# Picking two gathered rows per step by matmul from the first step to the last double step

## The chip, the cores and the metric

The kernel runs on one core of one Trainium2 chip. The metric is the device time of one execution in microseconds. Three runs of the kernel before took 1789.95 to 1790.13 us, with a median of 1790.06 us.

The core has five engines with their own instruction queues: TensorE (PE; its weight loads are listed apart as PEld), VectorE (DVE), ScalarE (ACT), GpSimd (POOL) and the SyncE queue (SP), which here only issues DMAs.

## The reference

A graph has N = 6250 nodes with 64 features and E = 206,250 edges, sorted by destination. There are four heads of 16 features.

```python
Qh = (x @ Wq.T + bq).reshape(n, H, D)
Kh = (x @ Wk.T + bk).reshape(n, H, D)
Vh = (x @ Wv.T + bv).reshape(n, H, D)
Ee = (edge_attr @ We.T + be).reshape(-1, H, D)
score = (Kh[src] * Qh[dst] * (1.0 / np.sqrt(D)) * Ee).sum(-1)
score = jnp.exp(jnp.clip(score, -5.0, 5.0))
msg = Vh[src] * score[..., None]
wV = jax.ops.segment_sum(msg, dst, num_segments=n)
out = _layernorm(x + wV.reshape(n, H * D), axis=-1)
```

Since the edges are sorted by destination, queries and sums are local. The sources are random, so k and v of each edge's source have to be fetched row by row.

## The kernel before, in words

**Tiles and steps.** 128 edges make a tile, one edge per partition; there are T = 1612 tiles. Eight tiles make a group (G = 8), 202 groups in all, the last with four tiles. `STEPS` cuts the groups into NS = 105 steps: 97 steps of two groups (16 tiles), then eight steps of one group.

**Where k and v of the sources come from.** There are four ways.

- Most tiles are gathered: `gather_kv` (line 400) issues one indirect DMA on POOL's queue for each tile, which reads 128 rows of the table `kv_tab` in DRAM.
- The first four groups (XG = 4, the tiles of steps 0 and 1) are gathered from x itself (line 230) while the tables are still being computed. The loop of line 370 then transposes them (L375), copies them to SBUF (L378) and multiplies them with the weights of k and v (L380, L382, L384).
- Of every sixth step from step 12, one tile is fetched row by row over SP's queue (`fetch_rows`, line 528).
- The last two tiles of a double step are *picked* by matmul. x lies in SBUF as three bf16 parts whose sum is the f32 value (`parts`, 50 blocks of 128 partitions). In step s, for both picked tiles of step s + 2, `sources` (line 460) writes a row of source numbers (ScalarE), `sources_turned` (469) transposes it on PE, `hots` (476) compares it on VectorE with the block numbers and so makes 50 one-hot matrices in two halves, and `picks` (486) multiplies them with the parts, 25 matmuls per half, so 100 in a step. In step s + 1, `picked` (494) adds the three parts, and `picked_turned` and `picked_kv` (502, 510) make k and v of the picked rows and write them into the step's buffer. The kernel before picks in steps 4 to 94 (`picks_in`, with M0 = 4 and LAST = NS - 11).

**Where the parts come from.** `table_parts` and `table_parts_rest` (444, 454) load x in blocks of eight over SP and split them on ScalarE and VectorE in the steps 0 to 3, after a memset of the whole tile (L427).

**Buffers of k and v.** `kvs` has KVB = 5 buffers, one per step in turn. In step s, after its message, `gather(s + 4)` is called. Step s + 5 uses the same buffer as step s, so the first of its gathers has to wait until the message of step s has read it. The gathers of groups 4 to 7 (steps 2 and 3) are issued ahead of the loop (line 406).

**The rest of a step.** The order on each engine is the order of the calls, written out by hand in the loop of line 708. `products` multiplies k with the queries and with the edge values (L602, L603), `scores` reduces, clips and exponentiates (L609, L611, L612), `message` multiplies v with the score (L619), `minus` splits the message into three bf16 parts (L622, L630, L632), `queries(s + 1)` (L595) makes the next step's queries, and `sums` (L638) and `add` (L652) collect the messages per destination in the next step. All PSUM tiles of the loop have one buffer each.

**The end.** When the last sums are there, `last_add` (693) adds them to the last block of 128 nodes; the layer norm of a block is `spreads`, `roots`, `scales` and `norm`. In the kernel before, `scales` and `norm` of the block before the last stand ahead of `last_add`.

The fallback behind `branch.Else()` for unsorted or widely spread destinations doesn't run with these inputs.

Of the kernel before, what the change touches and what calls it, by code (L numbers as in the profile page):

```python
# [37 lines left out]
CB = 10  # L38
KVB = 5
XG = 4  # L40
TB = 8
M0 = 4
PAD = N
SPARE = N + 1
TABLES = 4
# [8 lines left out]
def tiles_in(s):  # L54
    return sum(tiles_of(g) for g in groups_of(s))


def groups_of(s):
    return range(STEPS[s][0], STEPS[s][0] + STEPS[s][1])
# [1 line left out]

LAST = NS - 8 - 3


def picks_in(s):
    return M0 <= s <= LAST

# [31 lines left out]
def tile_gnn(ctx: ExitStack, tc: tile.TileContext, x, xT, wT, bias, beT, weT, eT, src, dst, dst_rows,  # L103
# [16 lines left out]
    def kv_of(g):  # L120

        s = max(s for s in range(NS) if STEPS[s][0] <= g)
        j = (g - STEPS[s][0]) * G
        return kvs[s % KVB][:, j:j + G, :]
# [29 lines left out]
    be_p = consts.tile([3, G, C], BF16, name="be_p")  # L154
    wkv = consts.tile([P, 2, 2 * C], F32, name="wkv")
    bkv_p = consts.tile([3, G // 2, 2 * C], BF16, name="bkv_p")
    minus_b = consts.tile([P, P], BF16, name="minus_b")

    acc = consts.tile([P, RING, 4, C], F32, name="acc")
# [24 lines left out]
    with tc.tile_pool(name="nodes", bufs=1) as nodes, \  # L184
# [182 lines left out]
            fetch_queries(g)  # L367


        for g in range(XG):  # L370
            for h in range(2):
                tp = npsum.tile([P, 2, P], F32, name="tp", bufs=2)
                for u in range(2):
                    j = 4 * h + 2 * u
                    nc.tensor.transpose(tp[:, u, :],  # L375
                                        XS[g][:, j:j + 2, :].rearrange("p j c -> p (j c)"), ident)
                xe = nodes.tile([P, 2, P], F32, name="xe", bufs=2)
                nc.scalar.activation(xe, tp, AF.Copy)  # L378
                pv = npsum.tile([P, 4, 2 * C], F32, name="pv", bufs=2)
                nc.tensor.matmul(pv, ones_b, bkv_p, start=True, stop=False, skip_group_check=True)  # L380
                for u in range(2):
                    nc.tensor.matmul(pv[:, 2 * u:2 * u + 2, :], xe[:, u, :], wkv, start=False,  # L382
                                     stop=u == 1, skip_group_check=True)
                nc.scalar.activation(kv_of(g)[:, 4 * h:4 * h + 4, :], pv, AF.Copy)  # L384

    def edge_values(pe, et, n):

# [6 lines left out]
    def keys(t0):  # L394

        n = min(KEYS, T - t0)
        nc.vector.tensor_scalar(key_i[:, :n], dst_i[:, t0:t0 + n], P - 1, None, op0=OP.bitwise_and)
        nc.vector.tensor_copy(key[:, t0:t0 + n], key_i[:, :n, None].to_broadcast([P, n, 2]))

    def gather_kv(g, j):  # L400
        t = g * G + j
        nc.gpsimd.indirect_dma_start(  # L402
            out=kv_of(g)[:, j, :], out_offset=None, in_=kv_tab[:, :],
            in_offset=bass.IndirectOffsetOnAxis(ap=src_i[:, t:t + 1], axis=0))

    for g in range(XG, 2 * KVB - 2):
        for j in range(G):
            gather_kv(g, j)

    rv = nc.values_load(n_wide[0:1, 0:1], min_val=0, max_val=NR2 * 4)  # L410

    with tc.If(rv == 0) as branch:

        with tc.tile_pool(name="work", bufs=2) as work, \
# [8 lines left out]
            pa = small[:, 4 * C:7 * C].rearrange("p (i c) -> p i c", i=3)  # L423
            nc.tensor.transpose(col, row_b[:, 0:1].to_broadcast([P, P]), ident_b)

            parts = accp.tile([P, NB, 3, C], BF16, name="parts")
            nc.vector.memset(parts, 0.0)  # L427
            NX = N // NB
            x_v = x.rearrange("(p b) c -> p b c", p=NX)
            n_picks = LAST - M0 + 1  # L430
            src_f = accp.tile([P, n_picks, 2], F32, name="src_f")
            t0 = (M0 + 3) * 2 * G - 2
            for i in range(2):
                nc.vector.tensor_copy(src_f[:, :, i],
                                      src_i[:, t0 + i:t0 + i + 2 * G * (n_picks - 1) + 1:2 * G])
            pick = fixed.tile([P, 4 * P], F32, name="pick")
            rows3 = pick[:, :6 * C].rearrange("p (k i c) -> p k i c", k=2, i=3)
            HOT, FAR, X = {}, {}, {}
# [2 lines left out]

                return ap.rearrange("p (a b) -> p a b", b=2)

            def table_parts(b):

                n = min(TB, NB - b)
                raw = work.tile([P, TB, C], F32, name="raw", bufs=1)
                nc.sync.dma_start(raw[:NX, :n], x_v[:, b:b + n, :])
                rest = pick[:NX, :n * C].rearrange("p (b c) -> p b c", b=n)
                nc.scalar.activation(rest, raw[:NX, :n], AF.Copy)  # L450
                nc.scalar.activation(parts[:NX, b:b + n, 0], raw[:NX, :n], AF.Copy)
                return rest

            def table_parts_rest(b, rest):
                n = min(TB, NB - b)
                nc.vector.tensor_sub(rest, rest, parts[:NX, b:b + n, 0])
                nc.scalar.activation(parts[:NX, b:b + n, 1], rest, AF.Copy)
                nc.vector.tensor_sub(parts[:NX, b:b + n, 2], rest, parts[:NX, b:b + n, 1])

            def sources(s, i):  # L460

                if picks_in(s):
                    FAR[s, i] = work.tile([P, P], BF16, name="far")
                    nc.scalar.activation(FAR[s, i], row50, AF.Identity,
                                         bias=src_f[:, s - M0, i:i + 1], scale=-1.0)

            def sources_turned(s, i):
                if picks_in(s):  # L470
# [39 lines left out]
            def picked_kv(s):  # L510
                if picks_in(s):
                    xe, kv = X.pop(s)
                    nc.tensor.matmul(kv, ones_b, bkv_p[:, :2], start=True, stop=False,
                                     skip_group_check=True)
                    nc.tensor.matmul(kv, xe, wkv, start=False, stop=True, skip_group_check=True)  # L515
                    nc.scalar.activation(kvs[(s + 2) % KVB][:, 2 * G - 2:, :], kv, AF.Copy)

            def gather(s):
                for g in groups_of(s):
                    for j in range(tiles_of(g)):  # L520
                        if is_rowed(s) and (g - STEPS[s][0]) * G + j == COLUMN:
                            continue
                        if not picks_in(s - 2) or g == STEPS[s][0] or j < G - 2:
                            gather_kv(g, j)

            RS, RK = {}, {}
# [53 lines left out]
            def onehot_edges(s):  # L580

                n, t0 = tiles_in(s), STEPS[s][0] * G
                OH[s] = work.tile([P, 2 * G, P], BF16, name="of")
                shape = [P, n, P // 2, 2]
                nc.vector.tensor_tensor(OH[s].rearrange("p t (a c) -> p t a c", c=2)[:, :n],  # L585
                                        pairs(col)[:, None].to_broadcast(shape),
                                        key[:, t0:t0 + n, None, :].to_broadcast(shape),
                                        op=OP.is_equal)
# [95 lines left out]
            def scales(lo, hi):  # L684
                nc.vector.reciprocal(rstd[:, lo:hi], rstd[:, lo:hi])

            def norm(b):
                nc.vector.tensor_scalar(y[:, b, :], y[:, b, :], stats[:, b, 0:1], rstd[:, b:b + 1],
                                        op0=OP.subtract, op1=OP.mult)
                n = P if b < BIG else REST  # L690
                nc.sync.dma_start(out[b * P:b * P + n, :], y[:n, b, :])
# [6 lines left out]
                                               op0=OP.mult, op1=OP.add)  # L698

            closed, scaled, normed = 0, 0, 0  # L700
            keys(0)
            for k, g in enumerate(groups_of(0)):
                onehot_rows(g, spread(g))
# [1 line left out]
                edges(0, k)  # L705
            queries(0)
            onehot_edges(0)
            for s in range(NS):
                more = s + 1 < NS
                for g in groups_of(s):  # L710
# [13 lines left out]
                sources_turned(s + 1, 0)  # L724
                if nexts[1:]:
                    onehot_rows(nexts[1], spread(nexts[1]))
                making = [b for b in range(s * 2 * TB, (s + 1) * 2 * TB, TB) if b < NB]
                if making:
                    rest = table_parts(making[0])
                prod = products(s)  # L730
                picked(s - 1)
                if more:
# [36 lines left out]
                if more:  # L769
# [9 lines left out]
                    for _ in range(3):  # L779
                        if normed < scaled:  # L780
                            norm(normed)
                            normed += 1
                for i, b in enumerate(making):
                    if i:
                        rest = table_parts(b)
                    table_parts_rest(b, rest)
            assert normed == B - 2
            sums(NS - 1)
            roots(B - 2, B - 1)
            close(B - 1)  # L790
            scales(B - 2, B - 1)
            norm(B - 2)
            last_add(NS - 1)
            spreads(B - 1)
            roots(B - 1, B)
            scales(B - 1, B)
            norm(B - 1)

    with branch.Else():

        sums = [dram.tile([NR, C], F32, name=f"sums{i}") for i in range(TABLES)]
        with tc.tile_pool(name="gconsts", bufs=1) as gc, \
                tc.tile_pool(name="gloads", bufs=3) as loads, \
                tc.tile_pool(name="ggath", bufs=4) as gath, \
                tc.tile_pool(name="gwork", bufs=2) as work, \
                tc.tile_pool(name="gpsum", bufs=2, space=bass.MemoryType.PSUM) as psum:
            zeros = gc.tile([P, NB * C], F32, name="zeros")
# [25 lines left out]
            def gather(g, j):  # L833
                if j == 0:
                    Q[g] = gath.tile([P, G, C], F32, name="gq")
                t = g * G + j
                if g >= 2 * KVB - 2:
                    gather_kv(g, j)
                nc.gpsimd.indirect_dma_start(
                    out=Q[g][:, j, :], out_offset=None, in_=q_tab[:, :],  # L840
                    in_offset=bass.IndirectOffsetOnAxis(ap=dst_i[:, t:t + 1], axis=0))
# [121 lines left out]
```

## Time and profile before

| what | value |
|---|---|
| median of three runs | 1790.06 us |
| the profiled execution | 1789.88 us, span 1788.0 us |
| PE busy / weight loads | 1638.5 us (92%) / 1369.6 us |
| DVE busy | 1481.6 us (83%) |
| ACT busy | 914.0 us (51%) |
| POOL busy | 1337.4 us (75%) |
| mean granted PE clock | 0.951 of full |
| kv gathers on POOL (L402) | 1383 of 944 ns |
| pick matmuls (L491) | 9100, 828.3 us busy in all |
| one-hot compares (L481) | 364 of 1813 ns |

The span runs from the first to the last instruction of the profiled execution; the execution's own time is 1.9 us longer. A row of the slices divides the span into 40 parts of 44.7 us and gives the busy share of each in tenths. In a group of instructions, the figures behind the first bar are total busy time and mean length in ns, and behind the second the engine's idle time just before them with what ended most of it. In the waits, the figures are total us, times, and the longest. Rows of the timeline begin with the start and the length in us; an idle time before the instruction and its releaser stand in brackets. Matmuls overlap, so their busy times add up to more than PE is really occupied.

### The profile page before, as it was taken

Reading aid. Unit: us, or ns where it says so; the run is one execution under the profiler, and the core shown is the slowest. Engines: PE = TensorE matmul, PEld = TensorE weight load, DVE = VectorE, ACT = ScalarE, POOL = GpSimd, SP = SyncE. Lnnn points to the kernel's source line nnn. Section 1 sums busy time; section 2 is a strip of 40 time slices with the busy share of each in tenths; the row PEclk is TensorE's granted clock in tenths of the full one; section 3 lists DMA queues with packets and bytes.
Section 4 is the critical chain, followed back from the end, with each engine's and each line's share of the span. In section 5 each row is a group of like instructions: output and inputs, shape, how many; then the busy total and the mean of one; then the engine's idle time right before and its main releaser. Section 6 shows DMA issues by size and latency. Waiting matters only on the chain.

```text
span 1788.0 us, 44286 instructions
## 1 busy us (share of the span) xinstructions
PE 1638.5 (92%) x15751; PEld 1369.6 (77%) x15751; DVE 1481.6 (83%) x1695; ACT 914.0 (51%) x1328; POOL 1337.4 (75%) x1427
## 2 busy tenths in 40 slices
PE   8978999999999998999999899999989998999864
PEld 8647888888888787787887778777877887787632
DVE  6459999999998898888889888888988888898654
ACT  3465555555554464454455445455544554455443
POOL 7777777777777777777777777777777777777774
PEclk9968999999999999999999999999999999999855
DMA  7443333333333333332333333323332333333331
GB/s 221 132 121 84 90 93 94 93 94 92 93 81 94 93 86 89 92 94 80 93 93 81 93 81 93 92 81 99 87 93 80 94 93 81 93 90 81 91 80 44
DMA packets 109970, 166.71 MB, mean 93 GB/s; under 512 B 69196, under 2 KB 71452, under 8 KB 109626
## 3 DMA queue, kind: packets, MB, share of 16 engines
q0 software_dynamic: 45280, 91.78, 19.4%
q1 hardware_dynamic: 64074, 71.01, 14.1%
q8 instruction: 125, 2.05, 0.5%
q10 hardware_dynamic: 384, 1.00, 0.3%
q14 instruction: 107, 0.88, 0.2%
HBM read 156.33 MB, written 7.33 MB: 92 GB/s over the span
## 4 chain that ended last, share of the span: by engine, by line
PE 38%; POOL 29%; issue 14%; DVE 13%; DMA 4%; ACT 3%; DVEq 0%; SPq 0%; POOLq 0%; ACTq 0%
POOL kv L402 29%; PE pick L491 18%; PE pe L391 5%; DVE hot L481 5%; DMA kv<-kv_tab,src_i 3%; PE pq L630 2%; PE small L638 2%; DVE prod L603 2%; DVE prod L602 2%; PE pb L555 2%; PE pe L388 2%; PE pb L515 1%; PE pq L595 1%; DVE pq L619 1%; PE ps L350 1%
## 5 line engine op out<-in xcount | busy, mean ns | idle before, releaser
L402 POOL DMA_INDIRECT kv<-kv_tab,src_i x1383 | 1305.3, 944 | 421.7 <-issue 399.8
L491 PE MATMUL pick<-parts,hot 128*128 128x192 bf16 x9100 | 828.3, 249 | 0.0
L491 PEld LDWEIGHTS <-hot 128*128 128x128 bf16 x9100 | 771.7, 99 | 38.1
L481 DVE TENSOR_TENSOR hot<-small,block 128x3200 bf16<-128x3200 bf16 x364 | 645.3, 1813 | 0.4 <-PE pick L491 0.4
L572 ACT ACTIVATE to<-pb,minus_row 126x1024 bf16<-126x1024 f32 x202 | 222.7, 1102 | 371.0 <-PE pb L555 367.2
L632 ACT ACTIVATE msg<-pq 128x1024 bf16<-128x1024 f32 (+2 forms) x210 | 207.6, 989 | 222.3 <-PE pq L630 222.3
L391 PEld LDWEIGHTS pe<-we_sb,et 128*128 128x128 f32 x1612 | 209.7, 203 | 133.4 <-issue 95.3
L602 DVE TENSOR_TENSOR prod<-kv,pq 128x1024 f32<-128x1024 f32 (+2 forms) x105 | 123.5, 1176 | 169.3 <-DMA kv<-kv_tab,src_i 52.0
L391 PE MATMUL pe<-we_sb,et 128*128 128x128 f32 x1612 | 250.3, 302 | 0.0
L577 ACT ACTIVATE to<-to,one_p 126x1024 bf16<-126x1024 bf16 x202 | 230.6, 1142 | 3.5
L638 PEld LDWEIGHTS <-of 128*128 128x128 bf16 x1612 | 145.3, 102 | 31.1 <-issue 7.9
L638 PE MATMUL small<-msg,of 128*128 128x192 bf16 x1612 | 161.9, 257 | 0.5 <-ACT msg L632 0.5
L388 PE MATMUL pe<-be_p,ones_b 3*128 3x512 bf16 x202 | 79.7, 395 | 86.3 <-DVE prod L603 86.1
L630 PE MATMUL pq<-msg,minus_b 128*128 128x512 bf16 x404 | 128.0, 396 | 33.1 <-ACT msg L622 19.5
L622 ACT ACTIVATE msg<-pq 128x1024 bf16<-128x1024 f32 (+2 forms) x105 | 103.8, 989 | 96.8 <-DVE pq L619 96.8
L609 DVE TENSOR_REDUCE small<-prod 128x64 f32<-128x1024 f32 (+2 forms) x105 | 123.6, 1177 | 14.5 <-PE small L471 8.8
L555 PE MATMUL pb<-key_rows,ident_b 112*128 112x512 bf16 x403 | 127.9, 400 | 2.8 <-ACT to L572 2.8
L603 DVE TENSOR_TENSOR prod<-prod,pe 128x1024 f32<-128x1024 f32 (+2 forms) x105 | 123.6, 1177 | 3.6
L619 DVE TENSOR_TENSOR pq<-kv,small 128x1024 f32<-128x1024 f32 (+2 forms) x105 | 123.4, 1175 | 1.4 <-ACT small L612 1.4
L585 DVE TENSOR_TENSOR of<-small,key 128x2048 bf16<-128x2048 bf16 (+2 forms) x105 | 122.9, 1171 | 0.3
L595 PEld LDWEIGHTS <-to 126*128 126x128 bf16 x1612 | 63.5, 101 | 25.3 <-issue 25.1
L612 ACT ACTIVATE small<-small 128x64 f32<-128x64 f32 (+2 forms) x105 | 21.7, 207 | 111.1 <-DVE small L611 109.2
(129 smaller groups left out, 996.4 us busy)
## 6 DMA issues: line engine op xcount, KB each, us to landing
et<-in_eT SPq DMA_DIRECT2D x100, 512.0 KB
rk<-kv_tab SPq DMA_DIRECT2D x1920, 0.5 KB
kv<-kv_tab,src_i POOLq DMA_INDIRECT x1383
qw<-q_tab SPq DMA_DIRECT2D x202, 15.8 KB
kv_tab<-kv_sb SPq DMA_DIRECT2D x5, 640.0 KB
q_tab<-q SPq DMA_DIRECT2D x5, 480.0 KB
acc<-in_x SPq DMA_DIRECT2D x48, 32.0 KB
out<-y SPq DMA_DIRECT2D x48, 32.0 KB
```

Source lines behind the costliest of these rows:

```text
L391: nc.tensor.matmul(pe[:, 2 * u:2 * u + 2, :], et[:, u, :], we_sb, start=False, stop=u == n // 2 - 1, skip_group_check=True)
L402: nc.gpsimd.indirect_dma_start(out=kv_of(g)[:, j, :], out_offset=None, in_=kv_tab[:, :], in_offset=bass.IndirectOffsetOnAxis(ap=src_i[:, t ...
L481: nc.vector.tensor_tensor(HOT[s, i, h].rearrange("p b (a c) -> p b a c", c=2), pairs(from_b[i])[:, None].to_broadcast(shape), block2[:, bl ...
L491: nc.tensor.matmul(rows3[:, i], hot[:, k, :], parts[:, b], start=b == 0, stop=b == NB - 1)
L555: nc.tensor.matmul(pb[:, b:b + 4, :], ident_b[:NR2, g // 2:g // 2 + 1].to_broadcast([NR2, P]), key_rows[:, g % 2, b * P:(b + 4) * P], star ...
L572: nc.scalar.activation(TO[g][:, :n, :], pb[:3 * W, :n, :], AF.Square, bias=minus_row3[:3 * W])
L577: nc.scalar.activation(TO[g][:, :n, :], TO[g][:, :n, :], AF.Relu, bias=one_p[:3 * W], scale=-1.0)
L602: nc.vector.tensor_mul(prod[:, :n, :], kvs[s % KVB][:, :n, :C], PQ[s][:, :n, :])
L603: nc.vector.tensor_mul(prod[:, :n, :], prod[:, :n, :], PE[s][:, :n, :])
L630: nc.tensor.matmul(msg[:, lo:hi, :], minus_b, M3[s][:, lo:hi, i, :], start=False, stop=True, skip_group_check=True)
L632: nc.scalar.activation(M3[s][:, :n, i + 1, :], msg[:, :n, :], AF.Copy)
L638: nc.tensor.matmul(PA[s], OH[s][:, j, :], M3[s][:, j], start=j == 0, stop=j == n - 1)
```

## The change

Three things change.

1. Picks are made in steps 0 to 96 instead of 4 to 94. The tiles of steps 2 to 5 and of the single-group steps 97 and 98 that were gathered are now picked: two tiles for each of six more steps. `is_picked` decides for the gathers ahead of the loop and in it. The sources of step 0 and the hots of its first tile are made ahead of the loop.
2. The parts of x are made before the loop, in the chunk that computes k and v of the first four groups: x, which lies transposed in SBUF already (`xT_sb`), is transposed back on PE, four blocks at a time, and split on ScalarE and VectorE. In that chunk the rows of the next half group are turned before k and v of the present one are computed. The loads of x over SP, the memset and the splitting inside steps 0 to 3 go.
3. At the end, `last_add`, `spreads` and `roots` of the last block stand ahead of `scales` and `norm` of the block before it.

The changes in the fallback only keep it consistent. The core of the diff:

```diff
-LAST = NS - 8 - 3
+LAST = NS - 8 - 1
 def picks_in(s):
-    return M0 <= s <= LAST
+    return 0 <= s <= LAST
+
+def is_picked(g, j):
+    s = max(s for s in range(NS) if STEPS[s][0] <= g)
+    return picks_in(s - 2) and g == groups_of(s)[-1] and j >= G - 2
...
+        def parts_of_x(b):
+            n = min(TB, NB - b)
+            px = npsum.tile([P, 2, 2 * C], F32, name="ps").rearrange("p i (j c) -> p (i j) c", j=2)
+            px = px[:, :n]
+            for u in range(n):
+                nc.tensor.transpose(px[:, u, :], xT_sb[:C, (b + u) * P:(b + u + 1) * P],
+                                    ident[:C, :C])
+            nc.scalar.activation(parts[:, b:b + n, 0], px, AF.Copy)
+            nc.vector.tensor_sub(px, px, parts[:, b:b + n, 0])
+            halves.append((px, b, n))
+
+        def rest_of_x():
+            px, b, n = halves.pop(0)
+            nc.scalar.activation(parts[:, b:b + n, 1], px, AF.Copy)
+            nc.vector.tensor_sub(parts[:, b:b + n, 2], px, parts[:, b:b + n, 1])
+
+        order = [(g, h) for g in range(XG) for h in range(2)]
+        blocks = list(range(0, NB, TB))
+        xe = x_turned(*order[0])
+        for i, gh in enumerate(order):
+            following = x_turned(*order[i + 1]) if i + 1 < len(order) else None
+            for b in blocks[2 * i:2 * i + 2]:
+                parts_of_x(b)
+            first_kv(*gh, xe)
+            xe = following
+            while halves:
+                rest_of_x()
...
     for g in range(XG, 2 * KVB - 2):
         for j in range(G):
-            gather_kv(g, j)
+            if not is_picked(g, j):
+                gather_kv(g, j)
...
-            parts = accp.tile([P, NB, 3, C], BF16, name="parts")
-            nc.vector.memset(parts, 0.0)
...
-                        if not picks_in(s - 2) or g == STEPS[s][0] or j < G - 2:
+                        if not is_picked(g, j):
                             gather_kv(g, j)
...
             closed, scaled, normed = 0, 0, 0
+            sources(0, 0)
+            sources_turned(0, 0)
             keys(0)
...
             queries(0)
             onehot_edges(0)
+            sources(0, 1)
+            sources(1, 0)
+            for h in range(2):
+                hots(0, 0, h)
             for s in range(NS):
...
-                making = [b for b in range(s * 2 * TB, (s + 1) * 2 * TB, TB) if b < NB]
-                if making:
-                    rest = table_parts(making[0])
...
-                for i, b in enumerate(making):
-                    if i:
-                        rest = table_parts(b)
-                    table_parts_rest(b, rest)
             assert normed == B - 2
             sums(NS - 1)
             roots(B - 2, B - 1)
             close(B - 1)
-            scales(B - 2, B - 1)
-            norm(B - 2)
             last_add(NS - 1)
             spreads(B - 1)
             roots(B - 1, B)
+            scales(B - 2, B - 1)
+            norm(B - 2)
             scales(B - 1, B)
             norm(B - 1)
```

`x_turned` and `first_kv` are the two halves of the old loop body of line 370 (transposes and first copy; matmuls and second copy). `TB`, the blocks split at a time, goes from 8 to 4.

## The prediction

> **What bounds the kernel now.** I read the busy table and the slices first, then the groups, then the waits and the table of windows.
>
> ```profile
> PE 1638.5 (92%) x15751; PEld 1369.6 (77%) x15751; DVE 1481.6 (83%) x1695; ACT 914.0 (51%) x1328; POOL 1337.4 (75%) x1427
> ...
> POOL 7777777777777777777777777777777777777774
> ...
> L402 POOL DMA_INDIRECT kv<-kv_tab,src_i x1383 | 1305.3, 944 | 421.7 <-issue 399.8
> L491 PE MATMUL pick<-parts,hot 128*128 128x192 bf16 x9100 | 828.3, 249 | 0.0
> ```
>
> By share of busy time PE leads. But POOL's digit is 7 in every slice from first to last, as only an engine that never waits has it. The waits explain the missing quarter:
>
> ```profile
> POOL kv L402 <- issue: 399.8, 1311, 0.3
> ```
>
> 1311 times 0.3 us in front of a gather while nothing was outstanding, and never longer: a gather occupies POOL for 0.944 us plus 0.3 us. The first kv gather starts at 43.04 us and the last at 1768.85, so one costs 1725.8/1382 = 1.249 us. POOL is the bound for the whole run; a step with two picks (14 gathers) is 17.5 us long on it. PE's own pace is shorter: where PE has arrears (160 to 366 us) its blocks of picks return every 15.7 us, and later the first product waits for the gather's DMA.
>
> ```profile
> 60.00:80.00 20.00, 19.31 (x48) 10.82 (x48) 2.44 (x1) 6.62 (x13) 15.12 (x17) 1.00 0.33 90
> 100.00:120.00 20.00, 13.62 (x67) 8.75 (x66) 12.73 (x15) 14.72 (x19) 15.12 (x17) 0.65 0.42 120
> 300.00:400.00 100.00, 100.00 (x1056) 85.58 (x1054) 93.55 (x99) 54.07 (x76) 75.54 (x81) 1.00 0.35 93
> ```
>
> Columns: window, length, busy PE, PEld, DVE, ACT, POOL, granted PE clock, DMA share, GB/s. POOL stays at 75.6% whether VectorE does 12% or 94%.
>
> **The change part by part.**
>
> *Gathers.* Picks go from 91 to 97 steps, so POOL loses 6 x 2 = 12 gathers, 15.0 us. Eight lie at the start (tiles of steps 2 to 5), four at the end (steps 97 and 98). The two ends have different covers, so I cost them apart: 8 x 1.249 = 10.0 us and 4 x 1.249 = 5.0 us at most.
>
> *The steps' added work.* Six steps get 100 pick matmuls (25 in 2.06 us: 8.2 us of PE) and four hots (1.81 us each, 7.25 us of DVE). In steps 0 to 3 they take the place of the table's parts, of a 4.06 us memset, and of waits: those steps now start their products at 84.97, 100.98, 117.00 and 133.22, 16.1 us apart, with PE at a clock of 0.61 to 0.65. With picks I give them the 15.7 us of later steps, within POOL's 17.5. So they cost nothing if PE runs at full clock; the rivals price the other case.
>
> A rule speaks against the added hots: the Trainium skill, "SBUF — State Buffer", section "SBUF: two separate sides", says that a VectorE operation in a two-port mode locks GpSimd out of a shared port, so that it can't write descriptors for its DMAs. If each of the 24 new hots held up POOL for its length, 24 x 1.81 = 43 us would be lost. The windows above show the gathers' pace unchanged at 94% VectorE; I take nothing.
>
> *Parts of x between k and v.* These are 50 transposes of 64x128, 13 ScalarE copies and 13 subtractions, twice each. No row shows these transposes. The nearest is the query matmul with the same stationary shape and the same 64 moving columns; from the chain of waits:
>
> ```profile
> 33.58 18.15 PE ps L350 x84
> ```
>
> 0.216 us each, 10.8 us for 50. The other bound is the 128-column transpose of line 375, two in 0.63 us: 0.31 each, 15.7 us. I take 0.216. ScalarE (4 x 0.38 + 0.38 + 0.60 = 2.5 us per half group) and DVE (about 1.7) stay under PE's 4.4. Turning the next half ahead of k and v saves part of this wait:
>
> ```profile
> 58.48 0.60 PE L380 MATMUL pv<-bkv_p,ones_b 3*128 3x512 bf16 x1
> 58.65 0.38 ACT L378 ACTIVATE xe<-tp 128x256 f32<-128x256 f32 x1
> 59.08 1.36 PEld L382 LDWEIGHTS pv<-wkv,xe 128*128 128x128 f32 x4 [0.51 <-ACT xe L378]
> ```
>
> Of the 0.51 us some 0.2 is the bias matmul's own; I take 0.3 x 8 = 2.4 us. So the step loop's prelude starts 8.4 us later (bounds 5 and 15.7). Behind the branch, PE now waits for the first "far" row (source copies, one ScalarE activation, one transpose) ahead of its spread: about 1.55 us. SP loses seven loads of x and only gets freer.
>
> *What is late next.* The gathers of step 5 write the buffer that step 0 read, so they wait for step 0's message:
>
> ```profile
> 90.33 1.23 DVE L619 TENSOR_TENSOR pq<-kv,small 128x1024 f32<-128x1024 f32 x1 [1.36 <-ACT small L612]
> ...
> 103.08 0.94 POOL L402 DMA_INDIRECT kv<-kv_tab,src_i  x1 [0.30 <-issue]
> ```
>
> Now the buffer is free at 91.56 and is wanted at 103.08: 11.5 us of slack. After, it is wanted 6 gathers earlier (2 + 2 + 2), at 43.04 + 42 x 1.25 = 95.6. The message ends at 91.56 + 8.4 + 1.55 - 0.9 (two part copies that stand before exp on ScalarE now) + 0.3 (source transposes in step 0) = 100.9. POOL stalls for 5.3 us, and all gathers behind it are late by that. Step 6 is wanted 17.5 us later, and message 1 should come 15.2 to 15.7 us after message 0: no second stall. Front: -10.0 + 5.3 = -4.7.
>
> *The end.* After step 96 the groups are single and the steps follow the chain product, score, message, two subtractions, queries. Starts of the first product of steps 100 to 104:
>
> ```profile
> 1738.05 0.69 DVE L602 TENSOR_TENSOR prod<-kv,pq 128x512 f32<-128x512 f32 x1 [2.59 <-PE pq L595]
> 1746.68 0.69 DVE L602 TENSOR_TENSOR prod<-kv,pq 128x512 f32<-128x512 f32 x1 [2.59 <-PE pq L595]
> 1756.58 0.69 DVE L602 TENSOR_TENSOR prod<-kv,pq 128x512 f32<-128x512 f32 x1 [4.27 <-PE small L638]
> 1766.65 0.69 DVE L602 TENSOR_TENSOR prod<-kv,pq 128x512 f32<-128x512 f32 x1 [4.72 <-PE small L638]
> 1774.05 0.42 DVE L602 TENSOR_TENSOR prod<-kv,pq 128x256 f32<-128x256 f32 x1 [3.31 <-PE pq L595]
> ```
>
> 8.63 us is the chain's own length (the product waits for queries); only the 9.9 and 10.07 wait for gathers. Earlier gathers can take those two down to 8.6: 2.8 us. The picks of step 96 put about 0.9 us back (a reduction of 0.55 and two k and v matmuls). So the four gathers give -1.9, not -5.0; the rest becomes slack on POOL.
>
> *Last sums first.* The last reduction now waits for another block's root: its table load ends at 1780.44 and the reduction starts at 1781.12, while the last sums on PE ended at 1780.00. Going first gains 1.07; the other block's reciprocal and norm then stand between the last root and its use, 0.3 back: -0.8.
>
> **Sum.** -4.7 - 1.9 - 0.8 = -7.4 us. The span goes from 1788.0 to 1780.6, the profiled execution's 1789.88 to 1782.5; the median of the runs, 1790.06, lies 0.2 above that execution: 1782.7 us.
>
> **Rivals.**
> A, no stall: the transposes cost half (0.107) or hide in gaps, and POOL never waits: -10.0 - 1.9 - 0.8 gives 1777.4; with the full 5.0 at the end, 1774.3. For it speaks that a weight load of line 375's transposes lasts 0.23 us where one of L350 lasts 0.33; against it, the delay would have to be under 3.1 us, and 1.55 of prelude come on top.
> B, no measurable change: 0.31 us per transpose and no gain from turning ahead make 15.7 us, 7.3 more, all stall: 1790.0. Line 375's row speaks for it, its twice as many columns against it.
> C, slower, PE's clock: the Trainium skill, "TensorE: Matmul & The Clock Gate", section "Part 1: The HAM clock gate", says that the array is throttled by default and only sustained activity releases it. At the 0.61 to 0.65 of the window from 100 to 120, the 8.2 us of picks take 13.4, and a step about 20.9, 3.4 over POOL's 17.5; four such steps stall POOL by 13.8 us: 1796.5. It decides from 19.4 us per step (7.4 lost). Against it: when picks begin at 150 us, 25 matmuls take 2.06 to 2.23 us at once, and the clock is 1.00 from 160 on; after the change PE is dense from 51 us on.
>
> **How the numbers follow.** My case has 0.64 (own range 1779.5 to 1786), A 0.13, B 0.14, C 0.09. A measurement of this kernel tells about 0.2% (3.6 us) from no change. Faster: my case, A, and a fraction of B, 0.80. Same: the rest of B and mild C, 0.12. Slower: 0.08. The range takes in A without the full end and most of B: 1776.5 to 1788.5.
>
> **What would show it.** The gather group falls to x1371 at 944 ns, the picks rise to 9700. One wait of POOL of about 5 us, near 96 us, for step 0's message (DVE, the line of the message's product), and none later; the last gather starts near 1768.85 - 15.0 + 5.3 = 1759. The chunk of k and v with transposes takes about 33 us instead of 24.6. PE's clock is near 1.00 between 100 and 140 us, and products come 15.7 us apart from step 0 to step 35 or so. In the last eight steps products wait for queries, none for a DMA. I am wrong if POOL doesn't wait at the start (A), waits repeatedly (C), or if the last product's lag behind the last gather doesn't grow by about 3 us.

## The result: 7.3 us faster, for partly other reasons

The changed kernel takes 1782.72 us (median of five runs, 1778.57 to 1783.07); the kernel before takes 1790.06 (1789.95 to 1790.29). The ratio is 0.9952, 95% interval 0.9938 to 0.9967. The profiled execution took 1782.72 us, its span is 1780.8 us; before it was 1788.0, so 7.2 us of span went. The prediction was 1782.7 us. The total is right, and two of its three terms are not: in this profile they are wrong by 3.3 and 3.7 us in opposite directions.

The busy table, the slices and the groups of the profile after, against the lines shown of before:

```profile
PE 1676.8 (94%) x16437; PEld 1416.1 (80%) x16437; DVE 1522.3 (85%) x1738; ACT 916.8 (51%) x1357; POOL 1326.2 (74%) x1415
...
POOL 7777777777777777777777777777777777777773
PEclk9999999999999999999999999999999999999965
...
L440 POOL DMA_INDIRECT kv<-kv_tab,src_i x1371 | 1294.2, 944 | 420.0 <-issue 395.0
L513 PE MATMUL pick<-parts,hot 128*128 128x192 bf16 x9700 | 882.9, 249 | 0.0
```

The gathers fall from 1383 to 1371 and still take 944 ns each; the picks rise from 9100 to 9700, and POOL keeps its 7 in every slice but the last. The added work on PE and VectorE did not slow a gather.

POOL's own instructions in order of time (start, duration, then in brackets the idle time ahead of it) show the stall that the prediction placed at 95.6 us:

```profile
96.26 0.94 POOL L440 DMA_INDIRECT kv<-kv_tab,src_i  x1 [0.84 <-DVE pq L642]
...
115.14 0.94 POOL L440 DMA_INDIRECT kv<-kv_tab,src_i  x1 [1.71 <-issue]
```

Every other kv gather has 0.30 to 0.32 in the brackets. The first of these is step 5's first gather behind message 0: 0.84 - 0.30 = 0.54 us lost. The second is step 6's first gather, which has to wait for message 1; that message ends on VectorE at 113.16 + 1.22 = 114.38 us. 1.41 us are lost there. The profile names no releaser for it; that it is message 1 follows from the buffers. Together 1.95 us, not 5.3, and at two places, not one. The last gather, before and after:

```profile
1768.85 0.94 POOL L402 DMA_INDIRECT kv<-kv_tab,src_i  x1 [0.30 <-issue]
```

```profile
1756.06 0.94 POOL L440 DMA_INDIRECT kv<-kv_tab,src_i  x1 [0.30 <-issue]
```

It starts 12.8 us earlier (12 gathers are 15.0 us; 15.0 - 1.95 = 13.0).

The end did not follow. The first product of step 96 before, and those of steps 96 to 100 and 104 after the change, on VectorE:

```profile
1696.65 1.22 DVE L602 TENSOR_TENSOR prod<-kv,pq 128x1024 f32<-128x1024 f32 x1 [7.05 <-ACT to L572]
```

```profile
1689.93 1.22 DVE L625 TENSOR_TENSOR prod<-kv,pq 128x1024 f32<-128x1024 f32 x1 [2.61 <-PE small L661]
1703.91 0.69 DVE L625 TENSOR_TENSOR prod<-kv,pq 128x512 f32<-128x512 f32 x1 [2.40 <-PE pick L513]
1714.79 0.69 DVE L625 TENSOR_TENSOR prod<-kv,pq 128x512 f32<-128x512 f32 x1 [3.94 <-ACT kv L539]
1725.34 0.68 DVE L625 TENSOR_TENSOR prod<-kv,pq 128x512 f32<-128x512 f32 x1
1734.54 0.69 DVE L625 TENSOR_TENSOR prod<-kv,pq 128x512 f32<-128x512 f32 x1 [2.49 <-PE pq L618]
...
1767.81 0.42 DVE L625 TENSOR_TENSOR prod<-kv,pq 128x256 f32<-128x256 f32 x1 [3.31 <-PE pq L618]
```

Product 97 waits for PE, which has the picks of step 96, and product 98 for the k and v that those picks make. Both waits are new. The first two of the four blocks of picks of step 96 in the changed kernel, and the queries of step 97 in the kernel without picks at the end (the first of the experiments):

```profile
1693.75 3.88 PE L513 MATMUL pick<-parts,hot 128*128 128x192 bf16 x25
1698.03 2.14 PE L513 MATMUL pick<-parts,hot 128*128 128x192 bf16 x24
```

```profile
1698.39 0.58 PE L618 MATMUL pq<-qw,to 126*128 126x64 bf16 x8 [1.11 <-ACT msg L655]
```

In the changed kernel a third block follows at 1701.36 us, and only then, at 1703.42, the queries of step 97. Without those picks the queries wait for the message alone. From product 96 to the last it takes 77.9 us; before it took 77.4 (1696.65 to 1774.05). So the 7.2 us of span are: product 96 comes 6.72 earlier, the eight steps to the last product are 0.48 longer, and from the last product to the end it is 0.96 shorter (12.99 against 13.95 us). So 10.0 - 1.95 = 8.05 of the front's 10.0 us reach the gathers (7.8 by the last gather's start: 12.8 less the 5.0 of the four gathers at the end), and 6.72 of those reach product 96.

### The profile page after: what moved, and what is told of

Its sections match the earlier page's. It is cut to its first block, busy times and chain, and to the rows that moved or that the text cites. A ratio compares the mean times of both kernels' runs of the same rounds, so it can differ in the third digit from the quotient of the medians.

```text
span 1780.8 us, 45728 instructions
## 1 busy us (share of the span) xinstructions
PE 1676.8 (94%) x16437; PEld 1416.1 (80%) x16437; DVE 1522.3 (85%) x1738; ACT 916.8 (51%) x1357; POOL 1326.2 (74%) x1415
## 5 line engine op out<-in xcount | busy, mean ns | idle before, releaser
L513 PE MATMUL pick<-parts,hot 128*128 128x192 bf16 x9700 | 882.9, 249 | 0.0
L513 PEld LDWEIGHTS <-hot 128*128 128x128 bf16 x9700 | 822.4, 99 | 40.5
L503 DVE TENSOR_TENSOR hot<-small,block 128x3200 bf16<-128x3200 bf16 x388 | 688.1, 1814 | 1.9 <-PE pick L513 1.8
L429 PEld LDWEIGHTS pe<-we_sb,et 128*128 128x128 f32 x1612 | 204.7, 199 | 114.1 <-issue 79.6
L429 PE MATMUL pe<-we_sb,et 128*128 128x128 f32 x1612 | 244.6, 297 | 0.0
L661 PEld LDWEIGHTS <-of 128*128 128x128 bf16 x1612 | 139.6, 99 | 28.2 <-issue 4.5
L661 PE MATMUL small<-msg,of 128*128 128x192 bf16 x1612 | 155.1, 250 | 0.5 <-ACT msg L655 0.5
L653 PE MATMUL pq<-msg,minus_b 128*128 128x512 bf16 x404 | 124.2, 386 | 18.4 <-ACT msg L645 11.5
L675 DVE SCALAR_TENSOR_TENSOR acc<-small,above,acc 128x192 f32<-128x192 f32 x103 | 43.0, 418 | 38.3 <-ACT small L635 37.2
```

What stands on the lines that cost most here:

```text
L429: nc.tensor.matmul(pe[:, 2 * u:2 * u + 2, :], et[:, u, :], we_sb, start=False, stop=u == n // 2 - 1, skip_group_check=True)
L503: nc.vector.tensor_tensor(HOT[s, i, h].rearrange("p b (a c) -> p b a c", c=2), pairs(from_b[i])[:, None].to_broadcast(shape), block2[:, bl ...
L513: nc.tensor.matmul(rows3[:, i], hot[:, k, :], parts[:, b], start=b == 0, stop=b == NB - 1)
L653: nc.tensor.matmul(msg[:, lo:hi, :], minus_b, M3[s][:, lo:hi, i, :], start=False, stop=True, skip_group_check=True)
L661: nc.tensor.matmul(PA[s], OH[s][:, j, :], M3[s][:, j], start=j == 0, stop=j == n - 1)
```

## The experiments

Theory T is this reading of the trace: the stall is 1.95 us, the front gives 8.05 at the gathers, the new order of the last sums gives about 1.0, and the two picks at the end give nothing or even cost up to the 1.8 us that are left over (8.05 + 0.96 - 7.2). Theory P is the prediction's: stall 5.3 (front -4.7), end -1.9, order -0.8. The kernel before stood beside each run.

### Without the two picks at the end

```
-LAST = NS - 8 - 1
+LAST = NS - 8 - 3
```

> The same kernel as no_end_picks, since in those four runs the kernel before itself took 3095 us and TensorE waited some 1481 us in front of the queries alone[...]: there POOL, whose gathers both theories are about, was not the bound, and neither theory is tested. Where POOL's gathers run back to back, T expects 1781.0 us, P 1784.6.

Measured: 1779.0 us (1778.7 to 1780.52; before 1790.1), ratio 0.9940, interval 0.9927 to 0.9954, span 1777.2 us. That is 5.6 us under P's number, 1784.6, and 2.0 under T's, 1781.0. By itself it doesn't decide between them, because something else moved as well, in the chunk that makes k and v of the first groups. PE's instructions there, in this kernel (start, duration, line):

```profile
56.74 2.08 PE L390 MATMUL pv<-wkv,xe 128*128 128x256 f32 x4
...
60.57 1.13 PE L390 MATMUL pv<-wkv,xe 128*128 128x256 f32 x4
...
70.50 1.13 PE L390 MATMUL pv<-wkv,xe 128*128 128x256 f32 x4
```

In the middle of the chunk PE's rate nearly doubles, in code that the changed kernel has too. (Below, 2.08 us for these four matmuls is called the half rate, and 1.13 us the full rate.) In the changed kernel's profile it does not:

```profile
56.61 2.08 PE L390 MATMUL pv<-wkv,xe 128*128 128x256 f32 x4
...
78.57 2.08 PE L390 MATMUL pv<-wkv,xe 128*128 128x256 f32 x4
```

So the chunk ends 9 us sooner here (71.63 against 80.65), product 0 starts at 81.67 us instead of 90.41, and no gather waits longer than 0.3 us. This run differs from the changed kernel in two things, the end's picks and the rate. Without any stall P would have it at 1784.6 - 5.3 = 1779.3, close to what was measured: the time alone fits P's end too. The next run sets the rate on purpose.

### A burst ahead of the chunk

40 bf16 matmuls of 128 x 128, whose result nobody reads, stand in front of the chunk of the changed kernel.

```
+        pb = npsum.tile([P, 2, 2 * C], F32, name="ps").rearrange("p i c -> p (i c)")
+        for k in range(40):
+            nc.tensor.matmul(pb[:, :P], ident_b, ident_b, start=True, stop=True)
         xe = x_turned(*order[0])
```

> The changed kernel with the burst of 40 bf16 matmuls ahead of the k/v chunk, once more, beside a kernel before that takes 1790 us. Reading of the trace: chunk some 18 us instead of 31.4, message 0 some 9 us earlier, no stall of POOL, 1782.7 - 1.95 = 1780.8 us, with less scatter than 1778.6 to 1783.1. The prediction on record (stall 5.3): 1777.4 us. Rival, that the end takes back what the front gives: 1782.7 us. Where the kernel before takes some 3090 us instead, [...]only the front's rows can be read.

Measured: 1778.92 us (1777.85 to 1779.91; before 1790.02), ratio 0.9936, interval 0.9923 to 0.9950, span 1777.9 us. The rival, 1782.7, falls: every run lies below it. P's number, 1777.4, and T's, 1780.8, lie 1.5 below and 1.9 above, so the rows have to decide. PE's instructions at the chunk:

```profile
51.50 3.58 PE L416 MATMUL ps<-ident_b 128*128 128x128 bf16 x40
...
56.41 1.13 PE L390 MATMUL pv<-wkv,xe 128*128 128x256 f32 x4
...
70.81 1.13 PE L390 MATMUL pv<-wkv,xe 128*128 128x256 f32 x4
```

3.6 us of burst, and every iteration runs at the full rate: PE needs 17.0 us for the chunk (54.92 to 71.94) where the changed kernel needs 30.7 (49.97 to 80.65). Message 0 starts at 86.14 us, 8.6 before the changed kernel's 94.76, though the chunk began 5.0 later. POOL never waits more than 0.3 us:

```profile
POOL kv L443 <- issue: 398.7, 1308, 0.3
POOL kv L443 <- DMA kv<-kv_tab,src_i: 9.8, 32, 0.3
```

The columns are what it waited for, the sum in us, how often, and the longest. With the stall gone the last gather starts at 1754.51, 1.55 us before the changed kernel's:

```profile
1754.51 0.94 POOL L443 DMA_INDIRECT kv<-kv_tab,src_i  x1 [0.30 <-issue]
```

The first kv gather came 0.27 later in this run (43.40 against 43.13 us), so the stall was worth about 1.8 to 1.95. A stall of 5.3 would have given more than three times that. The time came out 1.9 us under T's number. Half of that is in the profiled run: product 96 gains 2.45 us, not 1.55, and the way from it to the end another 0.45. The other half is that this profiled run, 1779.91 us, was the slowest of the five, 1.0 above their median.

Beside the kernel without picks at the end, whose chunk also ran mostly at the full rate, this settles the end. From the two kernels and the two of before and after:

| us | before | after | no end picks | burst |
|---|---|---|---|---|
| last gather starts | 1768.85 | 1756.06 | 1758.90 | 1754.51 |
| product 96 starts | 1696.65 | 1689.93 | 1686.75 | 1687.48 |
| last product starts | 1774.05 | 1767.81 | 1764.02 | 1765.00 |
| span | 1788.0 | 1780.8 | 1777.2 | 1777.9 |
| product 96 to last product | 77.40 | 77.88 | 77.27 | 77.52 |

The burst kernel's gathers are done 4.4 us before those of the kernel without end picks, and its last product comes 1.0 us after. With the picks or without, the eight short steps take 77.3 to 77.9 us. That they agree is not because the picks do nothing there; two effects cancel.

The kernel without end picks, the products of steps 97, 98 and 101 to 104:

```profile
1699.01 0.69 DVE L625 TENSOR_TENSOR prod<-kv,pq 128x512 f32<-128x512 f32 x1 [4.40 <-PE pq L618]
1708.80 0.69 DVE L625 TENSOR_TENSOR prod<-kv,pq 128x512 f32<-128x512 f32 x1 [3.25 <-PE pq L618]
...
1736.71 0.69 DVE L625 TENSOR_TENSOR prod<-kv,pq 128x512 f32<-128x512 f32 x1 [2.31 <-PE pq L618]
1746.61 0.69 DVE L625 TENSOR_TENSOR prod<-kv,pq 128x512 f32<-128x512 f32 x1 [4.23 <-PE small L661]
1756.62 0.69 DVE L625 TENSOR_TENSOR prod<-kv,pq 128x512 f32<-128x512 f32 x1 [4.66 <-PE small L661]
1764.02 0.42 DVE L625 TENSOR_TENSOR prod<-kv,pq 128x256 f32<-128x256 f32 x1 [3.30 <-PE pq L618]
```

And those of steps 97, 98, 101 and 102 in the burst kernel:

```profile
1701.71 0.69 DVE L628 TENSOR_TENSOR prod<-kv,pq 128x512 f32<-128x512 f32 x1 [2.40 <-DMA kv<-kv_tab,src_i]
1712.38 0.69 DVE L628 TENSOR_TENSOR prod<-kv,pq 128x512 f32<-128x512 f32 x1 [3.73 <-ACT kv L542]
...
1740.71 0.69 DVE L628 TENSOR_TENSOR prod<-kv,pq 128x512 f32<-128x512 f32 x1 [2.58 <-PE pq L621]
1749.27 0.69 DVE L628 TENSOR_TENSOR prod<-kv,pq 128x512 f32<-128x512 f32 x1 [2.53 <-PE pq L621]
```

Without the picks the two late steps of 9.9 and 10.0 us are still there; in the burst kernel they are 8.56 each, which is 2.8 us gained, just what the prediction says. But its first two steps are 14.23 and 10.67 us where the others are 12.26 and 9.79: 2.85 us lost. That is the term that the prediction had at 0.9. So the two kernels, both without a stall, take the same time, 1778.92 and 1779.0 us (runs over 2.1 and 1.8 us), where P's end would put 1.9 us between them.

### Nine runs with another bound

On three other chips the kernel before itself took 3076 to 3095 us, so a time from them says nothing about the change on a chip where it takes 1790. The waits of the kernel with the transposes made twice show what holds there, first POOL's and then PE's line of the page's groups and waits:

```profile
L440 POOL DMA_INDIRECT kv<-kv_tab,src_i x1371 | 1297.1, 946 | 1739.9 <-DVE pq L642 1297.8
```

```profile
PE pq L618 <- issue: 665.6, 504, 5.7
PE pick L513 <- issue: 232.1, 315, 2.2
```

POOL idles for 1740 us and waits for messages; PE waits 666 us ahead of the queries with nothing outstanding that the profile shows. POOL is not the bound there. Why PE waits is open.

The kernel without end picks, and one with the pick of step 95 alone (`LAST = NS - 8 - 2`):

> Picks end at step 94 as before (the changed kernel without its picks in steps 95 and 96). Theory T, read off the changed kernel's trace: the four gathers saved at the end don't pay, because the last eight steps are bound by their own chain and the picks of steps 95 and 96 lengthen it by more than the gathers take off; without them the end is as before: about 1781.0 us, 1.8 less than with them. Theory P, as predicted: the end picks gain 1.9 us, so without them it takes 1784.6.

> Picks end at step 95: two gathers of step 97 are saved, those of step 98 are not. T: what hurts is above all step 96 (its picks run partly at the low clock, and the product of step 98 waits for the picked k and v), so this lies at or below the kernel without end picks, 1779.5 to 1781. P: halfway between 1782.7 and 1784.6, 1783.7.

3119.95 us (ratio 1.0076, 1.0063 to 1.0088) and 3122.53 us (1.0082, 1.0069 to 1.0095). Neither theory was tested; the kernel with the pick of step 95 alone was not run where the kernel before takes 1790 us.

Picks in steps 4 to 96 alone (`return 4 <= s <= LAST`), with the end as changed:

> Picks in steps 4 to 96 only: the parts are still made ahead of the loop, the gathers of steps 2 to 5 stay on POOL. The front then has over 5 us of slack and costs nothing, so this shows the end alone (picks of 95 and 96, and the last sums first). T: +1.8 - 1.0, so 1790.9. P: -1.9 - 0.8, so 1787.4.

> Picks only in steps 4 to 96: the front's eight gathers come back (8 x 1.249 = 10.0 us), while the transposes for the parts of x, the two picks at the end and the new order of the last sums stay. This shows what the end's part is worth alone. Reading of the trace (stall 1.95 us, end picks don't pay): the stall has no cover to fall through, so 1782.7 + 10.0 - 1.95 = 1790.8 us, no gain at all over the kernel before. The prediction on record (stall 5.3, end -1.9, order -0.8): 1790.1 - 2.7 = 1787.4 us.

3103.44 us (ratio 1.0028, 1.0018 to 1.0037) and 3084.92 us (1.0032, 1.0022 to 1.0042). With two added pick steps, at the end, the kernel is 9 us slower than before here; with four, at the front (the kernel without end picks), it is 25 us slower. The changed kernel itself was not run on these chips; with the end's old order (below) it is 0.9% slower than the kernel before. Where the kernel takes 1790 us, the front's 10 us were not measured by taking its picks back; they rest on POOL's count and on product 96.

Three kernels of this group can be read in single rows, since rows of the same instructions last as long here as in the changed kernel: the four matmuls of the chunk 2.08 us, and an iteration 4.01. First the transposes, made twice:

```
-            for u in range(n):
+            for u in [*range(n), *range(n)]:
```

> Each of the 50 transposes of x is made twice (100 more or less of PE's work ahead of the loop, same result). T: the front stalls POOL already, so the added 50 x 0.131 us = 6.6 us come through whole: 1789.3. The record's size of a transpose (0.216) would give 10.8 us: 1793.5. Rival: POOL's short waits at the front are not what sets the time (a transfer or the steps behind absorb them): no change, 1782.7.

3128.74 us (ratio 1.0113, 1.0098 to 1.0128). In the chunk, at the half rate, an iteration goes from 4.01 to 4.87 us; its transposes stand in these two rows, the first of the changed kernel, the second of this one:

```profile
55.03 1.11 PE L401 MATMUL ps<-ident,xT_sb 64*128 64x64 f32 x8
```

```profile
116.24 1.97 PE L401 MATMUL ps<-ident,xT_sb 64*128 64x64 f32 x16
```

Eight more cost 0.86 us, 0.108 each. Second, with 13 matmuls of 256 columns in their place, so that the parts hold another value:

```
-            for u in range(n):
+            nc.tensor.matmul(px, ones_b, be_p[:, :n, :], start=True, stop=True)
+            for u in range(0):
                 nc.tensor.transpose(px[:, u, :], ...        (the call goes on)
```

> The 50 transposes that turn x for its parts are replaced by 13 matmuls of 256 columns (one for each group of four blocks; the parts then hold another value than x, all later work is the same). The chunk loses 50 x 0.13 - 13 x 0.30 = 2.6 us by the trace, 50 x 0.216 - 3.9 = 6.9 by the prediction's duration. Reading of the trace: message 0 comes 2.6 us earlier, POOL's waits of 0.54 and 1.41 us go, 1782.7 - 1.95 = 1780.8 us. The prediction on record: its stall of 5.3 goes whole, 1777.4 us. Rival, that the end swallows what the front gives: 1782.7 us.

3099.24 us (ratio 1.0072, 1.0057 to 1.0088). An iteration takes 3.40 us, of which its two matmuls take 0.40 (117.13 to 117.53); the remaining 3.00 is what an iteration takes without any parts in the kernel before, 3.04 (53.01 to 56.05). So turning the next half ahead saves at most 0.04 us an iteration, and eight transposes add 0.97 us, 0.121 each, and 50 of them 6.1.

Third, the changed kernel with the end's old order:

```
+            scales(B - 2, B - 1)
+            norm(B - 2)
             last_add(NS - 1)
             spreads(B - 1)
             roots(B - 1, B)
-            scales(B - 2, B - 1)
-            norm(B - 2)
```

> The changed kernel with the end's old order: scales and layer norm of the block before the last go ahead of the last sums again. Prediction and trace agree on the mechanism: 0.8 (prediction) to 1.0 us (trace: last product to end 12.99 against 13.95) slower, 1783.5 to 1783.7 us. Rival, that the order is hidden behind another wait: 1782.7 us. If this lies under the scatter of the changed kernel's own runs (1778.6 to 1783.1) only the profile's distance from the last product to the end decides: 13.0 or 13.95 us.

3102.51 us (ratio 1.0088, 1.0072 to 1.0104): its runs lie over 8 us apart and can't show 1 us. The end's rows can. VectorE in the old order:

```profile
3086.61 0.42 DVE L642 TENSOR_TENSOR pq<-kv,small 128x256 f32<-128x256 f32 x1
...
3090.68 0.16 DVE L708 RECIPROCAL rstd<-rstd 128x1 f32<-128x1 f32 x1 [2.00 <-ACT rstd L705]
3090.88 0.31 DVE L711 TENSOR_SCALAR y<-y,stats,rstd 128x64 f32<-128x64 f32 x1
3091.11 0.35 DVE L719 TENSOR_REDUCE t<-small 128x64 f32<-128x192 f32 x1
...
3092.92 0.32 DVE L711 TENSOR_SCALAR y<-y,stats,rstd 128x64 f32<-128x64 f32 x1
```

And in the new order, of the kernel with 13 matmuls on the same chip (its lines are one further down):

```profile
3086.76 0.42 DVE L643 TENSOR_TENSOR pq<-kv,small 128x256 f32<-128x256 f32 x1
...
3090.17 0.36 DVE L720 TENSOR_REDUCE t<-small 128x64 f32<-128x192 f32 x1 [1.34 <-PE small L662]
...
3092.04 0.32 DVE L712 TENSOR_SCALAR y<-y,stats,rstd 128x64 f32<-128x64 f32 x1
```

From the last message to the last norm it is 6.31 us in the old order, with a wait of 2.00 for the root, and 5.28 in the new one, with a wait for the sums alone: 1.03 us.

The burst went to two of these chips first:

> 40 matmuls of 128 x 128 in bf16, whose result nobody reads, go ahead of the k/v chunk[...]. They ask whether TensorE's rate in the chunk, which doubled in the middle of it in one kernel's profile (2.08 us for four matmuls, then 1.13) and not in the changed kernel's, is what sets POOL's stall. If the burst brings the full rate: the chunk takes 17 to 20 us instead of 31.4, message 0 comes 7 us or more earlier even after the burst, no stall, 1780.8 us or less (1779 as the kernel without picks at the end). If it does not: everything behind it is 4.3 us later, and POOL's waits grow by 4.3: 1787.0 us. The prediction on record has full rate only from the prelude on and expects the second.

> The changed kernel with the burst of 40 bf16 matmuls ahead of the k/v chunk (3.9 us), which brought TensorE's full rate there (1.13 us instead of 2.08 for the four matmuls of an iteration). The chunk then takes some 18 us instead of 31.4, message 0 comes some 9 us earlier, and POOL has no stall. Reading of the trace (stall 1.95, and the two picks at the end give nothing): 1782.7 - 1.95 = 1780.8 us, above the 1779.0 of the kernel without picks at the end, and the runs scatter less than 1778.6 to 1783.1, since the scatter came from whether the rate rose in the chunk by itself. The prediction on record (stall 5.3): 1777.4 us. Rival, that the end takes back what the front gives: 1782.7 us.

3100.65 us (ratio 1.0079, 1.0065 to 1.0093) and 3119.71 us (1.0082, 1.0068 to 1.0096). The first of the two expectations can be read in the chunk: the iteration takes 2.23 us behind the burst (the four matmuls 1.13), and 4.01 without it in the kernel with the old end order (2.08). The burst lifts the rate on these chips too, in the first five of the eight iterations on both. Could the rate have risen there by chance? In the ten profiles without a burst the first iteration always has 2.07 to 2.08 us for its four matmuls, and in only two does a later one reach 1.13; in the three with the burst it is 1.13 from the first iteration on.

## Why the prediction was right, and where it was not

*Gathers, 8 x 1.249 and 4 x 1.249.* Right in size: 12 fewer, 944 ns each, no slower under VectorE at 85%. The rule on two-port modes that the prediction weighed doesn't reach the added compares: the same page of the Trainium skill, "SBUF — State Buffer", section "Who interferes with whom", says that `tensor_tensor`, which they are, has no such mode. The burst run agrees: without a stall POOL's longest wait over 1371 gathers is 0.3 us.

*Transposes, 0.216 each.* Wrong by almost half: 0.11 to 0.12 us at the half rate, up to 6.1 for 50, by the iterations with and without them. *Turning the next half ahead, -2.4.* Nothing of it came: at most 0.3 us by the run with 13 matmuls. The chunk grew by 6.1 us, from 24.6 to 30.7, where some 33 were predicted. The two misses partly cancel: 8.4 predicted, 6.1 measured. Rival A named half the duration, and with it a stall of nearly nothing.

*POOL's stall, 5.3.* The place was right (95.6 predicted, 95.7 by the trace), the size not. In the sum for message 0's end, 100.9, the chunk gave 2.3 less, the prelude 1.1 instead of 1.55, and the chunk started 1.8 us earlier than before, which the prediction had not looked for. Message 0 ended at 96.0. *No second stall* was wrong: message 1 came 18.4 us after message 0, not 15.2 to 15.7. The first block of picks ran at the half rate:

```profile
95.78 4.21 PE L513 MATMUL pick<-parts,hot 128*128 128x192 bf16 x25
```

Later blocks take 2.23, so the half rate cost 2.0 us: rival C in one block instead of four steps. In the burst kernel this block took 2.71, and message 1 came 16.9 us after message 0, 1.5 less for 1.5 less of picks. The rest of the difference to 15.7, about 1 us, is unexplained. From product 2 to product 16, the steps are 14.5 to 17.3 us apart, within POOL's 17.5. Front: -8.05 at the gathers where -4.7 was predicted.

*The end, -1.9.* This is the step that failed. Its gain was as predicted (2.8 us in the steps of 9.9 and 10.07). Its price, "about 0.9", counted the reduction and two matmuls of the picked k and v, and left out that three of the four blocks of picks of step 96 stand on PE ahead of the queries of step 97, and that product 98 waits for their result. Those two steps became 2.85 us longer in the burst kernel, whose picks of step 96 all ran at the full rate (2.23 us a block), and the sum is zero. In the profile of the changed kernel product 96 moreover waited for PE, 1.0 to 1.3 us behind what the gathers gave it. In the burst kernel, with the same end, it came 0.1 to 0.2 us behind them (counted back from the last gather, 56 gathers of 1.249 us), so the picks alone don't explain this, and its cause is open. The prediction's own sign fails with this step: the last product's lag behind the last gather was to grow by about 3 us, and it grew by 6.55 (5.20 before, 11.75 after).

*Last sums first, -0.8.* Right: 0.96 in the trace, 1.03 between the two orders on one chip.

So the total was met because a front taken 3.3 us too poor and an end taken 3.7 us too good cancel; that is luck. Of the 3.7, the experiments show 1.9 (the end gives nothing); the rest is 0.48 in the eight steps and the late product 96. The number depended on PE's rate too: in the changed kernel's profile the chunk ran at the half rate, and its five runs scatter over 4.5 us. With the rate lifted the median is 1778.92, and the five runs scatter over 2.1 us. That the scatter is the rate's is argued, not shown, since only the profiled runs show the rate, and the kernel without end picks scatters over 1.8 us with no burst.

The two best kernels, the burst (1778.92) and the one without end picks (1779.0), each beat the kernel before by 0.6%. Their intervals overlap with the changed kernel's own. Both together were not run.

## What to carry to other kernels

Work taken off the bounding engine pays only in steps that still wait for that engine: of the 5.0 us of gathers saved at the end, 2.8 could pay, in two of the eight last steps. When a cheap step is added to an engine that the tail waits for, ask what stands behind all of its instructions in that engine's order, not only behind its last ones. A term that meets the total deserves as much checking as one that misses it: measure each term at its own place.

## What the runs showed of the hardware

TensorE can be busy without a gap in the profile (where ends of matmuls are modelled) for 45 us, from 35 to 80 in the changed kernel, and stay at half rate: four matmuls of 128x256 take 2.08 us, where at the full rate they take 1.13. Two windows of the changed kernel (window, length, busy PE, PEld, DVE, ACT, POOL, granted clock, DMA share, GB/s):

```profile
45.00:50.00 5.00, 5.00 (x27) 4.85 (x26) 2.95 (x12) 2.60 (x13) 3.78 (x5) 1.00 0.88 326
70.00:75.00 5.00, 5.00 (x19) 3.12 (x18) 1.52 (x4) 2.21 (x7) 3.78 (x5) 1.00 0.20 52
```

and of the kernel with the burst:

```profile
65.00:70.00 5.00, 5.00 (x30) 3.47 (x29) 3.39 (x10) 4.49 (x15) 3.78 (x5) 1.00 0.22 58
75.00:80.00 5.00, 5.00 (x17) 3.23 (x17) 4.20 (x3) 3.83 (x4) 3.78 (x5) 0.50 0.19 52
```

The Trainium skill, "TensorE: Matmul & The Clock Gate", section "Part 1: The HAM clock gate", has the array throttled until it is active for some 4 us. The burst agrees: 3.6 us of bf16 matmuls are enough. The f32 matmuls ahead of the chunk and in it, PE full from 35 us on, are not; there the measurement decides. Which of their properties matters (the type, the 64 or 65 rows, the 64 columns) was not tried.

The column of the granted clock does not tell this: it says 1.00 at 70 us in the first kernel, where four matmuls take 2.08 us, and 1.00 at 65 us in the second, where they take 1.13. In these two profiles it falls below 1.00 only after the rate has once been full. Early in a run the rate is read from a matmul's duration.
